# A cross-attention block on one core: the empty TensorE instructions taken out of a software-pipelined step, and its rows put in another order

## The chip, the cores and the metric

The kernel runs on one core of a Trainium2 chip. That core has five engines that run on their own and meet through semaphores: TensorE (PE, whose weight loads the profile lists apart as PEld), VectorE (DVE), ScalarE (ACT), GpSimd (POOL), and SyncE (SP), which here only issues DMAs. The metric is the device time of one launch in microseconds (us). The time before the change is the median of three runs.

## The reference

128 sequences of 128 tokens, 256 features, all in float32. The queries come from `x`, keys and values from `ctx_1024`; 16 heads of 16 features; the mask lets a token see only earlier ones, and the first token's attention is set to zero. Then an output projection, a residual and a layer norm, a ReLU network with 1024 hidden features, a residual and a second layer norm.

```python
q = (query @ Wq + bq);  k = (key @ Wk + bk);  v = (values @ Wv + bv)      # 16 heads of 16
scores = einsum('bhqd,bhkd->bhqk', q, k) / sqrt(16)
scores = where(j < i, scores, -1e30);  attn = softmax(scores);  attn[:, :, 0, :] = 0
ctx = einsum('bhqk,bhkd->bhqd', attn, v)
x = layer_norm(query + ctx @ Wo + bo, ln1_g, ln1_b)
out = layer_norm(x + relu(x @ W1 + b1) @ W2 + b2, ln2_g, ln2_b)
```

## The kernel before

**Pairs and steps.** The work is cut into 64 pairs of sequences. A step handles one pair's attention scores and, beside them, later parts of earlier pairs: step `p` computes the scores and the softmax of pair `p`, the queries and keys of pair `p+1`, the values of `p`, the weighted sum and the output projection of `p-2`, the first hidden layer of `p-3` or `p-4`, the second of `p-4` or `p-5`, and the second layer norm of `p-6`. Pairs 0 to 6 are handled by functions written out one by one (`third` to `sixth`), pair 63 by `last_step` and what follows it. Pairs 7 to 62 run through `step(p)`, 56 times; the loop goes on for two more rounds in which only late rows are left.

**Order.** The engines' order is manual: each engine executes its instructions in the order in which the program states them. In `step` that order is the string `ORDER`. Each word is a key of `OPS`; `-1` or `-2` behind a word means that the row is run for the pair of one or two steps earlier. So `ORDER` fixes the order on all engines at once, and what an engine does is the sub-list of its own keys. Semaphores are set by the framework, from what reads and writes what.

**The keys that matter here.**

- `weigh` (PE, lines 574 and 584): the probabilities times the values, 96 small matmul records, into PSUM bank 7. `context` (DVE, lines 600 and 605): three instructions that take bank 7, multiply by the inverse sums and write `cxT`.
- `scores` (PE, line 428): 64 records into all eight banks, in eight groups. Strips 2 and 3 of the array go first into banks 4 and 5, strips 0 and 1 into banks 0 and 1, and so on; the last two groups are those of strips 0 and 1 into banks 6 and 7.
- `maskB2`, `maskB3`, `maskA` (DVE, lines 452 and 444): bank 4, bank 5, banks 6 and 7. `add0` to `add3`, `max0` to `max3` (DVE, lines 1873 and 1879): mask and row maximum in banks 0 to 3. `eh0` to `eh7` and `el0` to `el7` (ACT, line 920): the exponentials of two heads each with their sums. `recip`, `turni` (DVE, lines 499 and 504): the inverse sums and their transposition; `turn0` to `turn2` (DVE, line 521): transposition of the probabilities; `turnx` (line 1935): of the normed rows. `br0` to `br3` (SP, line 540): sixteen DMAs that bring what was transposed from `turned` to `brought`, across partitions.
- Products by seven multiplications in place of eight (Strassen-Winograd), each of which has rows on PE and a chain of evacuations behind it. `v1` to `v4`, `o1` to `o4`, `q1` to `q4`, `k1` to `k4` (values in bank 4, output projection in bank 5, queries in bank 7, keys in bank 3): the row with 1 has three products, with 2 two, with 3 and 4 one. `h1` to `h7` (first hidden layer, banks 0, 1 and 2) and `w1` to `w7` (second layer, bank 6): one product of four matmuls each. A float32 matmul of 128x128x128 is two records, so a row `h` or `w` has eight records and a step has 168 such records beside `weigh` and `scores`.
- The evacuations add into, or copy out of, the same banks: `ok ok2 oa ob or` and `wk wk2 wa wb wr` (DVE, line 1327), `ka kb kr` (DVE, lines 1256, 1259, 1262), `qa qb qr` (DVE), `va vb vf vr` (DVE), `hk hk2 hk5` (ACT, lines 1402 to 1408), `hb ha hf` (DVE, lines 1414, 1411, 1417), `re0` (DVE, line 1431) and `re1` to `re3` (ACT, line 1433, ReLU out of banks 0 and 1), `ro0` to `ro3` (ACT, line 1421), `ks` and `ks2` (ACT line 1267 and POOL line 1272: keys spread over two halves, after `kr`). The sums that Strassen needs are built on POOL: `hs`, `xs`, `oc`, `cc`, `xc`.
- In the loop a product that adds onto an earlier one in the same bank stands behind the evacuation that reads the earlier one: `h4` behind `ha`, `h7` behind `hk2`, `k3` behind `kk2`.

**Empty instructions.** Behind each row of products, `step` puts some empty TensorE instructions (line 240, `nc.tensor.nop`): the dictionary `EMPTY` gives 4 or 5 for an `h` or `w` row and 2 or 3 for the others, 104 in a step. `LEAD` could put some ahead of a step and is empty.

Of the kernel before, what the change touches and what calls it, by code (L numbers as in the profile page):

```python
# [19 lines left out]
def tile_cross_attention_block(  # L20
# [83 lines left out]
    def weight(w, name):  # L104
        n = w.shape[0] // P
        t = const.tile([P, n, w.shape[1]], F32, tag=name, name=name)
        nc.sync.dma_start(t, w.rearrange("(k p) n -> p k n", p=P))
        return t
# [18 lines left out]
    wk = weight(Wk, "wk")  # L127
# [28 lines left out]
    w1 = weight(W1, "w1")  # L156
# [3 lines left out]
    w2 = weight(W2, "w2")  # L160
# [77 lines left out]
    def empty(n):  # L238
        for _ in range(n):
            nc.tensor.nop(hint="pad", nofuse=True)  # L240
# [1819 lines left out]
    for n in range(3):  # L2060
        OPS[f"turn{n}"] = lambda p, n=n: turn(p, n < 2, n % 2)

    ORDER = """
        weigh re0-2 res1-2 turn2-1 re2-2 re3-2 re1-2 context norm2-1 scores hs2-1 turni-1 vs-1
        maskB3 br2 add0 oc0 o1 ro0-2 maskB2 oc2 maskA ro2-2 finish1-1 v1 ro3-2 max0 ro1-2 q1 ok
        vk0 eh1 oc1 lowmax w1-1 hs0-1 qk br3 w2-1 vk1 add1 eh0 xs2-1 max1 el6 v2 hs1-1 stats2
        w5-1 eh3 add3 oc3 h2-1 eh2 max3 br1 hs3-1 wk-1 vk2 el5 o2 tokc-1 v3 eh7 xc2-1 h1-1 ok2
        add2 xc3-1 eh6 max2 cc0 q2 res0 vf el4 o3 br0 va w3-1 ob hk-1 oa vb eh4 cc1 w6-1 hb-1
        xs0-1 el0 cc2 o4 k1 wk2-1 xs1-1 qk2 or tokx el7 finish2-1 load w7-1 stats1 eh5 q3 means
        v4 kk h6-1 qa xc0 wb-1 el1 cc3 qb k2 deviations vr el3 wa-1 h5-1 turn1 kk2 loadx hk2-1  # L2070
        w4-1 xs3-1 store-1 norm1 turn0 addbo k3 h7-1 hk5-1 ka kb el2 xc1 turnx q4 k4 h3-1 ha-1
        kr qr h4-1 ks recip ks2 hf-1 wr-1
    """.split()

    EMPTY = {'w1': 5, 'h1': 4, 'w2': 5, 'h2': 5, 'w3': 5, 'h3': 4, 'w4': 5, 'h4': 5, 'w5': 5, 'h5': 4, 'w6': 5, 'h6': 5, 'w7': 4, 'h7': 5, 'v1': 3, 'o1': 2, 'q1': 2, 'k1': 3, 'v2': 2, 'o2': 2, 'q2': 3, 'k2': 2, 'v3': 2, 'o3': 3, 'q3': 2, 'k3': 3, 'v4': 2, 'o4': 2, 'q4': 3, 'k4': 2}
    LEAD = {}

    def step(p):

        empty(LEAD.get(p, 0))  # L2080
        for key in ORDER:
            key, late = (key.split("-") + ["0"])[:2]
            q = p - int(late)
            if FIRST <= q < NP - 1:
                OPS[key](q)
                if key in EMPTY:
                    empty(EMPTY[key])

    FIRST = 7

# [50 lines left out]
    for p in range(FIRST, NP - 1 + late):  # L2141
        step(p)
# [4 lines left out]
    p = NP - 1  # L2147
# [124 lines left out]
    means = small.tile([P, 2, 2], F32, tag="mvl", name="mv_last", bufs=1)  # L2272
# [83 lines left out]
```

## Time and profile before

| what | us |
|---|---|
| median of three runs (1507.5 to 1510.52) | 1508.35 |
| the profiled execution, its own time | 1508.16 |
| its span, first to last instruction | 1506.2 |
| busy: PE 1478.2, PEld 1405.8, DVE 1418.2, ACT 1294.9, POOL 1317.1 | share of the span 98, 93, 94, 86, 87% |

The profile is one execution. A busy share is an average over stages; rows of the timeline give start and length of one instruction (or of several alike that follow each other, with their count), and in square brackets the idle time before it with what ended it. PE rows are matmul records whose ends are modelled, so the distance between starts says more than their lengths. DVE and ACT instructions overlap a little with the next on the same engine, so here too starts are compared. The chain of waits is followed back from the last instruction: at each step to what released it.

### The profile page before, as it was taken

The page shows a single profiled execution, that of the slowest core. Times are in us where ns is not written, and L with a number is a line of the kernel's source. Part 1 is how long each engine was busy: PE and PEld are TensorE (multiplying, and loading weights), DVE is VectorE, ACT ScalarE, POOL GpSimd, SP SyncE. Part 2 cuts the span into 40 slices and gives each one's busy share as a digit, 9 for nine tenths or more (in the row PEclk, how much of TensorE's full clock was granted, in tenths as well). Part 3 has the DMA queues.
Part 4 walks back from the last instruction along what each step waited for, and adds up shares of the span by engine and source line. Part 5 has one row for each costly group of instructions (what it writes and reads, how often), then busy time and mean ns, then how long its engine had stood idle before and what let it go on. Part 6 is the DMA issues. An engine that isn't in the chain of part 4 may idle for free.

```text
span 1506.2 us, 62177 instructions
## 1 busy us (share of the span) xinstructions
PE 1478.2 (98%) x20711; PEld 1405.8 (93%) x20711; DVE 1418.2 (94%) x3397; ACT 1294.9 (86%) x5445; POOL 1317.1 (87%) x1877
## 2 busy tenths in 40 slices
PE   9998899999999999999999999999999999999898
PEld 7887899999999999999999999999999999999888
DVE  7997899999999999999999999999999999999567
ACT  6568799999999999999999899999999999999553
POOL 6876798999999899899899899899899899899667
PEclk9999799999999999999999999999999999999999
DMA  9366666766666666676665676676676676665251
GB/s 199 86 125 136 141 147 135 150 136 137 147 152 137 144 139 139 142 153 141 139 145 132 142 159 133 141 148 133 139 161 139 134 149 137 137 153 121 52 133 50
DMA packets 351320, 205.66 MB, mean 137 GB/s; under 512 B 277808, under 2 KB 319024, under 8 KB 351024
## 3 DMA queue, kind: packets, MB, share of 16 engines
q1 hardware_dynamic: 348736, 199.58, 61.7%
q8 instruction: 188, 3.08, 1.0%
q10 hardware_dynamic: 2288, 2.11, 0.6%
q14 instruction: 108, 0.88, 0.2%
HBM read 55.06 MB, written 18.09 MB: 49 GB/s over the span
## 4 chain that ended last, share of the span: by engine, by line
PE 32%; DVE 29%; SPq 16%; POOL 7%; ACT 7%; DMA 5%; issue 4%; DVEq 0%; POOLq 0%; ACTq 0%
PE banks L1175 19%; SPq L540 15%; DVE turned L521 9%; PE banks L1392 5%; ACT hT L1433 4%; PE banks L428 4%; DMA brought<-turned 3%; DVE hT L1411 2%; POOL kT L1272 2%; POOL hS L1868 2%; DVE t L1327 2%; DVE hT L1431 2%; DVE bsa L1900 1%; DVE kr L1259 1%; DVE xT L277 1%
## 5 line engine op out<-in xcount | busy, mean ns | idle before, releaser
L920 ACT ACTIVATE sm<-banks,nmx 128x128 f32<-128x128 f32 x944 | 352.4, 418 | 7.5 <-DVE nmx L903 7.5
L920 ACT ACTIVATE sm<-sm,nmx 128x64 f32<-128x64 f32 x944 | 344.8, 416 | 0.0
L920 ACT ACTIVATION_READ_ACCUMULATOR sm<-sm,nmx 128x1 f32 x944 | 251.8, 267 | 0.0
L920 ACT ACTIVATION_READ_ACCUMULATOR sm<-banks,nmx 128x1 f32 x944 | 242.4, 257 | 0.0
L521 DVE STREAM_TRANSPOSE turned<-sm 128x1024 f32<-128x1024 f32 x186 | 222.5, 1222 | 6.0 <-DMA brought<-turned 4.2
L1175 PE MATMUL banks<-wt,hS 128*128 128x128 f32 x1344 | 178.5, 276 | 0.4 <-DVE t L1327 0.4
L1392 PE MATMUL banks<-xS,w1t 128*128 128x128 f32 x1344 | 177.3, 275 | 0.0
L1868 POOL TENSOR_TENSOR hS<-hT 128x512 f32<-128x512 f32 x112 | 142.9, 1276 | 30.5 <-ACT hT L1433 29.6
L1175 PEld LDWEIGHTS banks<-wt,hS 128*128 128x128 f32 x1344 | 164.4, 193 | 0.6 <-DVE t L1327 0.6
L1392 PEld LDWEIGHTS banks<-xS,w1t 128*128 128x128 f32 x1344 | 163.5, 192 | 0.0
L1879 DVE TENSOR_REDUCE nmx<-banks 128x4 f32<-128x512 f32 x224 | 153.8, 687 | 5.7
L428 PE MATMUL banks<-kT,qT 32*64 32x256 f32 (+1 forms) x3840 | 123.7, 335 | 6.2 <-DVE t L1446 0.8
L428 PEld LDWEIGHTS banks<-kT,qT 32*64 32x64 f32 x3840 | 90.0, 132 | 31.2 <-ACT hT L1433 17.2
L1392 PE MATMUL banks<-brought,w 128*128 128x128 f32 x896 | 118.3, 275 | 0.0
L1175 PE MATMUL banks<-w,hT 128*128 128x128 f32 x896 | 110.8, 276 | 3.4 <-ACT hT L1421 2.0
L1433 ACT ACTIVATE hT<-banks,b1e_c 128x256 f32<-128x256 f32 x168 | 67.4, 472 | 50.9 <-DVE hT L1431 50.9
L1175 PEld LDWEIGHTS banks<-w,hT 128*128 128x128 f32 x896 | 105.4, 193 | 4.2 <-ACT hT L1421 2.4
L1392 PEld LDWEIGHTS banks<-brought,w 128*128 128x128 f32 x896 | 109.2, 192 | 0.0
L1272 POOL TENSOR_TENSOR kT<-kr,half 128x512 f32<-128x512 f32 x56 | 58.2, 1040 | 52.6 <-DVE kr L1262 52.6
L1421 ACT ACTIVATE hT<-hT,b1e_c 128x256 f32<-128x256 f32 x224 | 95.6, 497 | 0.7
L1873 DVE TENSOR_TENSOR banks<-banks,neg 128x256 f32<-128x256 f32 x224 | 94.0, 420 | 0.2
L691 ACT ACTIVATE x<-t,nb,sd 128x256 f32<-128x256 f32 x126 | 69.0, 596 | 23.7 <-POOL nb L1919 12.0
(330 smaller groups left out, 4947.4 us busy)
## 6 DMA issues: line engine op xcount, KB each, us to landing
brought<-turned SPq DMA_DIRECT2D x936, 128.0 KB, 2.4
out_dram<-t SPq DMA_DIRECT2D x63, 256.0 KB, 4.8
xb<-in_x_dram SPq DMA_DIRECT2D x124, 128.0 KB, 3.7
cb<-in_ctx_dram SPq DMA_DIRECT2D x124, 128.0 KB, 3.7
x<-in_x_dram SPq DMA_DIRECT2D x31, 512.0 KB, 5.7
brought<-turned SPq DMA_DIRECT2D x40, 96.0 KB, 2.2
w<-in_L_xattn_W_dram SPq DMA_DIRECT2D x2, 1024.0 KB, 8.3
brought<-turned ACTq DMA_DIRECT2D x8, 128.0 KB, 5.0
```

Of the source, the lines that this page charges most:

```text
L428: nc.tensor.matmul(st["sps", hi][r][s * HP : (s + 1) * HP, m * 2 * n : (m + 1) * 2 * n].rearrange("p (e j) -> p e j", e=2), st["qT"][strip ...
L521: nc.vector.transpose(turned[:, :, at : at + 256].rearrange("p j (n a) -> p n j a", a=32), states[p]["sm", hi].rearrange("p h j -> p (h j) ...
L540: queue.dma_start(brought_all[32 * j : 32 * j + 32, i, at], turned_all[32 * i : 32 * i + 32, j * ROW + at.start : j * ROW + at.stop],)
L920: nc.scalar.activation(sm[:, h, :], src, AF.Exp, bias=nmx[:, h : h + 1], scale=1.0, **({"accum_out": st["su"][:, at : at + 1]} if summed e ...
L1175: nc.tensor.matmul(out, left(k) if self.depth > 1 else left, right(k) if self.depth > 1 else right, start=(n == 1 and k == 0), stop=(k == ...
L1272: nc.gpsimd.tensor_tensor(self.kT[:, :, 1, :], self.k, half[:, 1:2, None].to_broadcast([P, KC, TP]), ALU.mult)
L1392: nc.tensor.matmul(ps[:, i * P : (i + 1) * P].rearrange("p (n a) -> p n a", a=32), left(i), right, start=(n in (1, 2, 5) and i == 0), stop ...
L1421: nc.scalar.activation(self.hT[:, f, at], self.hT[:, f, at] if src is None else src, AF.Relu, bias=b1e_c[:, f : f + 1], scale=1.0,)
L1433: nc.scalar.activation(out, src, AF.Relu, bias=bias, scale=1.0)
L1868: nc.gpsimd.tensor_tensor(c[:, n], left, right, how)
L1873: nc.vector.tensor_tensor(ps[:, :, HP:], ps[:, :, HP:], neg[:, 1, None, :].to_broadcast([P, 4, HP]), ALU.add)
L1879: nc.vector.tensor_reduce(states[p]["nmx", 1][:, 4 * b : 4 * b + 4], banks[:, b].rearrange("p (n j) -> p n j", j=P), AX.X, ALU.max, negate ...
```

## The change

The dictionaries `EMPTY` and `LEAD` and the calls of `empty` in `step` go: 104 TensorE instructions in each of 56 steps. `ORDER` is replaced by another order of the same keys. The lag of some keys changes, so that the same work stands on the other side of a step's border: `re0`, `re1`, `res1`, `turn2`, `turni` and `norm2` move from the start of a step to the end of the one before; `hf`, `wr`, `ks`, `ks2` and `xc1` move from the end of a step to the start of the next; `load` and `res0` come a step later than before, `xc2` a little earlier. On PE `v1` now comes ahead of `o1`, and the last rows are `h7 q4 v4 k3 h4 k4 h3` (before: `k3 h7 q4 k4 h3 h4`). On DVE the end of a step is `ha kb ka turnx qr re0 vr kr turn1`, and the next begins with `hf wr context maskB2 add0 maskB3 maskA` (before: it ended with `ka kb turnx ha kr qr recip hf wr` and the next began with `re0 turn2 context turni maskB3 add0 maskB2 maskA`).

```diff
-        weigh re0-2 res1-2 turn2-1 re2-2 re3-2 re1-2 context norm2-1 scores hs2-1 turni-1 vs-1
-        maskB3 br2 add0 oc0 o1 ro0-2 maskB2 oc2 maskA ro2-2 finish1-1 v1 ro3-2 max0 ro1-2 q1 ok
-        vk0 eh1 oc1 lowmax w1-1 hs0-1 qk br3 w2-1 vk1 add1 eh0 xs2-1 max1 el6 v2 hs1-1 stats2
-        w5-1 eh3 add3 oc3 h2-1 eh2 max3 br1 hs3-1 wk-1 vk2 el5 o2 tokc-1 v3 eh7 xc2-1 h1-1 ok2
-        add2 xc3-1 eh6 max2 cc0 q2 res0 vf el4 o3 br0 va w3-1 ob hk-1 oa vb eh4 cc1 w6-1 hb-1
-        xs0-1 el0 cc2 o4 k1 wk2-1 xs1-1 qk2 or tokx el7 finish2-1 load w7-1 stats1 eh5 q3 means
-        v4 kk h6-1 qa xc0 wb-1 el1 cc3 qb k2 deviations vr el3 wa-1 h5-1 turn1 kk2 loadx hk2-1
-        w4-1 xs3-1 store-1 norm1 turn0 addbo k3 h7-1 hk5-1 ka kb el2 xc1 turnx q4 k4 h3-1 ha-1
-        kr qr h4-1 ks recip ks2 hf-1 wr-1
+        weigh ks-1 ks2-1 re3-2 hf-2 re2-2 vs-1 wr-2 context scores hs2-1 ro0-2 br3 maskB2 ro2-2
+        add0 oc0 ro1-2 maskB3 v1 xc1-1 ro3-2 maskA o1 max0 hs0-1 vk1 q1 lowmax eh0 br2 w1-1 oc2
+        eh1 xs0-1 add1 tokc-1 w2-1 oc1 vk0 qk xc3-1 max1 el4 xs1-1 w5-1 add2 oc3 eh2 add3 hs1-1
+        h2-1 max2 br0 eh3 max3 v2 el6 res0-1 ok h1-1 wk-1 eh7 tokx o2 hs3-1 vk2 eh4 q2 br1 ok2
+        v3 stats2 hk-1 w6-1 finish1-1 eh5 hb-1 o3 qk2 vb w3-1 el2 vf addbo ob oa eh6 q3 o4 wk2-1
+        h6-1 va el0 qa cc0 or stats1 cc1 el7 loadx w7-1 cc3 qb load-1 el5 means xs2-1 k1 wa-1
+        el1 deviations wb-1 h5-1 turn0 el3 w4-1 kk cc2 recip hk2-1 turn2 xc2 k2 xc0 hk5-1 h7-1
+        finish2-1 kk2 turni norm1 q4 v4 ha-1 xs3-1 k3 store-1 norm2 res1-1 kb h4-1 ka turnx k4
+        qr h3-1 re0-1 vr kr re1-1 turn1
...
-    EMPTY = {'w1': 5, 'h1': 4, 'w2': 5, 'h2': 5, 'w3': 5, 'h3': 4, 'w4': 5, 'h4': 5, 'w5': 5, 'h5': 4, 'w6': 5, 'h6': 5, 'w7': 4, 'h7': 5, 'v1': 3, 'o1': 2, 'q1': 2, 'k1': 3, 'v2': 2, 'o2': 2, 'q2': 3, 'k2': 2, 'v3': 2, 'o3': 3, 'q3': 2, 'k3': 3, 'v4': 2, 'o4': 2, 'q4': 3, 'k4': 2}
-    LEAD = {}
-
     def step(p):
 
-        empty(LEAD.get(p, 0))
         for key in ORDER:
             key, late = (key.split("-") + ["0"])[:2]
             q = p - int(late)
             if FIRST <= q < NP - 1:
                 OPS[key](q)
-                if key in EMPTY:
-                    empty(EMPTY[key])
```

## The prediction

> **What bounds the kernel now.** I first read the busy shares, then the chain of waits, then one step of the timeline, engine by engine.
>
> ```profile
> PE 1478.2 (98%) x20711; PEld 1405.8 (93%) x20711; DVE 1418.2 (94%) x3397; ACT 1294.9 (86%) x5445; POOL 1317.1 (87%) x1877
> ```
>
> Two engines are nearly full, so the shares alone don't say which one sets the time. The chain does:
>
> ```profile
> 722.65 2.28 DVE turned L521 x2
> 731.48 5.35 PE banks L1175 x46
> 739.28 2.47 PE banks L1175 x22
> 745.13 2.28 DVE turned L521 x2
> ```
>
> It changes between PE and DVE in each step, and a step takes 745.13 - 722.65 = 22.48 us. So neither engine's sum sets the step, but a loop through both. The step's PE rows show where it closes.
>
> ```profile
> 705.41 0.43 PE L574 MATMUL banks<-brought,vd 128*32 128x64 f32 x16
> ...
> 706.89 2.11 PE L428 MATMUL banks<-kT,qT 32*64 32x128 f32 x64
> 708.94 0.71 PE L1175 MATMUL banks<-wo,cxT 128*128 128x128 f32 x4
> 709.49 0.39 PE L1175 MATMUL banks<-wot,oc 128*128 128x128 f32 x2
> ...
> 717.31 1.06 PE L1175 MATMUL banks<-w,hS 128*128 128x128 f32 x8
> 718.20 1.06 PE L1175 MATMUL banks<-wt,hS 128*128 128x128 f32 x8
> ```
>
> ```profile
> 707.40 1.35 PEld L428 LDWEIGHTS banks<-kT,qT 32*64 32x64 f32 x56 [0.31 <-ACT hT L1433]
> 708.94 0.52 PEld L1175 LDWEIGHTS banks<-wo,cxT 128*128 128x128 f32 x4 [0.19 <-DVE sm L452]
> ```
>
> From 709.49 to `w6` at 718.20 lie 78 records in 8.71 us, 0.1117 us each, without a gap; the first four of `o1` take 0.55, 0.10 more than that. PE loses time in `scores` alone: 0.31 us until `re1` has left banks 0 and 1, and 0.19 until `maskB3` has left bank 5, which is where DVE holds it.
>
> ```profile
> 708.50 0.38 DVE L452 TENSOR_TENSOR sm<-banks,neg 128x256 f32<-128x256 f32 x1
> ...
> 719.29 0.29 DVE L1327 TENSOR_TENSOR t<-banks,x1b 128x128 f32<-128x128 f32 x1
> ...
> 722.17 0.28 DVE L1311 COPY vz<-banks 128x128 f32<-128x128 f32 x1
> 722.37 0.28 DVE L1327 TENSOR_TENSOR t<-banks,t 128x128 f32<-128x128 f32 x1
> 722.57 2.36 DVE L521 STREAM_TRANSPOSE turned<-sm 128x1024 f32<-128x1024 f32 x2
> 724.88 0.29 DVE L1256 TENSOR_TENSOR kr<-banks,kr 128x128 f32<-128x128 f32 x1
> 725.08 0.41 DVE L1259 TENSOR_TENSOR kr<-banks,kr 128x256 f32<-128x256 f32 x1
> 725.41 0.70 DVE L1935 STREAM_TRANSPOSE turned<-x 128x512 f32<-128x512 f32 x1
> 726.04 0.65 DVE L1411 TENSOR_TENSOR hT<-banks,hT 128x512 f32<-128x512 f32 x1
> 726.61 0.33 DVE L1262 TENSOR_SCALAR kr<-banks,bk_c 128x128 f32<-128x128 f32 x1
> 726.87 0.34 DVE L1226 TENSOR_SCALAR qT<-banks,bqs_c 128x128 f32<-128x128 f32 x1
> 727.12 0.34 DVE L499 RECIPROCAL rs<-su 128x32 f32<-128x32 f32 x1
> 727.38 0.63 DVE L1417 TENSOR_TENSOR hT<-banks,hT 128x512 f32<-128x512 f32 x1
> 727.93 0.28 DVE L1327 TENSOR_TENSOR t<-banks,x1b 128x128 f32<-128x128 f32 x1
> 728.12 0.47 DVE L1431 TENSOR_SCALAR hT<-banks,b1e_c 128x256 f32<-128x256 f32 x1
> 728.51 1.23 DVE L521 STREAM_TRANSPOSE turned<-sm 128x1024 f32<-128x1024 f32 x1
> 729.67 0.38 DVE L600 TENSOR_TENSOR cxT<-banks,brought 128x256 f32<-128x256 f32 x1
> 729.98 0.47 DVE L605 TENSOR_TENSOR cxT<-banks,brought 128x124 f32<-128x124 f32 x2
> ```
>
> `w6` ends at 718.20 + 0.89 = 719.09 and `wk2` starts 0.20 later. From there DVE runs without a break, through all the rows shown, up to `maskB3` of the next step; it ends 22.48 after 708.50 + 0.38 = 708.88, and `o1` starts 0.06 after it. That is the loop of today: `o1` to `w6` on PE, `wk2` to `maskB3` on DVE. The same rows give the measures for the new order: 0.20 us from the end of a product to the DVE instruction that waits for it, 0.06 back, and DVE's distances from start to start.
>
> **The change part by part.**
>
> **The 104 empty instructions.** I put them at nothing.
>
> ```profile
> L240 PEldq NOP  x6292: 13/13/13, 1.1 to 1491.8; - x197
> ```
>
> Five stand behind `w3`, yet `w6` starts 0.89 after it, eight records' time, as between any two rows. The sequencer takes them while the array works off what is queued; that queue is their cover. Without it 104 of 13 ns would be worth 1.35 us a step, 72 us in all; that is the bound on one side. I see nothing by which taking them out costs time.
>
> **Work that moves but isn't on the loop.** No instruction of another engine is added or removed, so every engine's sum stays. The sixteen DMAs of `br` now start behind `context` and not behind `turni`:
>
> ```profile
> SPq L540 <- DVE turned L504: 397.0, 55, 9.6
> ```
>
> SP sat 397.0/55 = 7.2 us a step waiting for it, so its queue has room for `loadx`, `load` and `store`, which follow; what they bring is wanted a step later. The old `add`-`max` pairs, each of which waits for itself on DVE, are pulled apart; DVE gains there, but in the middle of the step, where in the new order it waits for products anyway. I put both at nothing; what ACT and POOL do in between I take as covered by their 14 and 13% of idle time.
>
> **What waits for what.**
>
> ```profile
> 727.04 0.72 ACT L1267 ACTIVATE kT<-kr,half 128x512 f32<-128x512 f32 x1 [0.64 <-DVE kr L1262]
> 728.63 1.20 ACT L1433 ACTIVATE hT<-banks,b1e_c 128x256 f32<-128x256 f32 x3 [0.87 <-DVE hT L1431]
> ```
>
> `re2` (the first of the three on ACT) waits for `re0` on DVE, though both only read, and other columns: what touches the same bank on another engine waits, in the program's order. And `ks` starts 727.04 - 726.61 = 0.43 after `kr`.
>
> **The new loop.** In the new order `v1` is the first product behind `scores`; from it to `h7` PE has 144 records. Behind `h7` comes `ha`, and behind `ha`, in order on DVE, all that ends in `context`. The last two groups of `scores` overwrite bank 7, where `context` reads, so they wait for it, and `v1` stands behind them on PE, with everything else that PE has. The terms:
>
> 1. `v1` to the end of `h7`: 144 x 0.1117 + 0.10 = 16.18.
> 2. To the start of `ha`: 0.20.
> 3. DVE from `ha` to `context`: `ha` 0.57, `kb` 0.33, `ka` 0.20, `turnx` 0.63, `qr` 0.25, `re0` 0.39, `vr` 0.20, `kr` 0.26, `turn1` 2.31/2 = 1.16, `hf` 0.55, `wr` 0.19: together 4.73.
> 4. `kb` reads bank 3, where `k3` stands ahead of it in the program, in other columns: as with `re2`, it waits. `k3` ends `q4 v4 k3`, six records or 0.67, behind `h7`, and 0.20 later `kb` may start, 0.87 behind `h7`; `ha` lets it start at 0.20 + 0.57 = 0.77. So 0.10 more.
> 5. `context`: 729.67 to 729.98 + 0.47 = 730.45, so 0.78; release 0.06.
> 6. The last two groups of `scores`:
>
> ```profile
> L428 PE MATMUL banks<-kT,qT x3840: 267/374/684, 81.5 to 1425.7; 32*64 32x128 f32 x97, 32*64 32x256 f32 x95
> ```
>
> 128 columns more take 374 - 267 = 107 ns. Two groups are four records of 128 columns one behind the other: 3 x 0.107 + 0.267 = 0.59. A third of an unhindered `scores` (below) would be 0.53; with a first-row cost like that of `o1` it is 0.69. I take 0.59.
>
> Sum: 16.18 + 0.20 + 4.73 + 0.10 + 0.78 + 0.06 + 0.59 = 22.64 us, 0.16 more than 22.48.
>
> Is PE early enough to feel that wait?
>
> ```profile
> 144.46 1.67 PE L428 MATMUL banks<-kT,qT 32*64 32x128 f32 x64
> 146.06 0.71 PE L1175 MATMUL banks<-wo,cxT 128*128 128x128 f32 x4
> ```
>
> Here, in the first step of the loop, `scores` waits for nothing and takes 1.60. Counted from the start of `ha`: `h4` may start at 0.65 + 0.06 = 0.71; `h4 k4 h3` are 18 records or 2.01; `weigh` starts 0.09 behind a row like these and takes 1.48 (705.41 to 706.89); and 1.60 - 0.59 = 1.01 of `scores` later PE stands before bank 7, at 0.71 + 2.01 + 0.09 + 1.48 + 1.01 = 5.30. DVE releases it at 4.83 + 0.78 + 0.06 = 5.67, so PE has to wait. ACT is no earlier than DVE: `kr` starts at 2.67, `ks` at 3.10, `re3` and `re2` follow it (0.72, a third of 1.20 and 0.47) and end by 4.66, and from there strips 0 and 1 need what they need today, 708.94 - 707.40 = 1.54, less the last 0.59: 5.67 with the release, or some 0.1 less, since ACT's instructions overlap. So two paths of about one length hold `v1`.
>
> The step repeats in full 53 times (56, less the first two, while late rows are missing, and the last): 53 x 0.16 = 8.5 us. Against the profiled execution's own 1508.16 that is 1516.7; the median of the runs is 0.2 higher, which I leave out.
>
> A rule of the Trainium skill bears on term 4. PSUM — Partial Sum Buffer, section "PSUM bank collisions raise a hardware error", says that no two engines may be in the same bank and quadrant at once, reads included, and that one guards by bank and not by address; the row of `re2` agrees. By it the step is 22.64. Guarded by address, `kb`, whose columns `k2` has finished, would not wait for `k3`: 22.54, and 1508.16 + 53 x 0.06 = 1511.3.
>
> **The rivals.**
>
> *`context` comes in time and the step gets shorter.* If DVE and ACT have bank 7 and banks 0 and 1 free when PE gets there, `v1` waits only for `maskB2`, one instruction behind `context`: that is 0.31 + 0.47 - 0.08 (the overlap seen between rows) = 0.70, its own 0.38 and 0.06. Terms 5 and 6 then become 1.14 in place of 1.43: 22.35, and 1508.16 - 53 x 0.13 = 1501.3. It decides as soon as the eleven rows of term 3, and `kr` with `ks` among them, take about 0.4 less than I sum (5.67 against 5.30). For it: `re0` and `turn2` no longer stand between `wr` and `context`, and `re1` is taken before the step's border. Against it: `turn1`, with 1.16 the longest row, stands there in their place. Were PE to meet no wait at all, its step would be 22.48 - (2.05 - 1.60) = 22.03 (2.05 is 706.89 to 708.94), and the time 1484.3.
>
> *It makes no difference.* The loop comes out within 0.06 of 22.48, for instance with no wait at `kb` and 0.53 for the groups (22.48): 1505 to 1511.
>
> *A wait between `hf` and `re2`.* Both write `hT`; the new order is `re3 hf re2`. If one waits for the other, `re2` starts behind `hf`, at 0.57 + 0.10 + 0.33 + 0.20 + 0.63 + 0.25 + 0.39 + 0.20 + 0.26 + 1.16 + 0.63 = 4.72 after `ha`, takes 0.47, and `scores` goes on from there to `v1` as after the 0.31 of today, in 708.94 - 707.40 = 1.54: 6.73 for terms 3 to 6 in place of 6.26, so 23.11, and 1541.6. Against it: they write other columns.
>
> *The empty instructions did hold something*: up to 72 us faster, by the bound above. Nothing in the rows speaks for it.
>
> **How the numbers follow.** The loop of 22.64: 0.62. No difference: 0.15. The shorter step: 0.16, and 0.02 for the empty instructions. `re2` behind `hf`: 0.05. The likeliest one's own range is 22.54 to 22.74 a step, 1511 to 1522. The range for 8 in 10 takes in no difference and part of the shorter step: 1503 to 1523. 0.2% or 3 us is about what a measurement of this kernel can tell from no change; all of the loop's range lies above 1511.2, so slower has 0.67, the same 0.15, faster 0.18.
>
> **What would show it.** In the changed profile: the step in the chain at 22.6; no row in which PE waits 0.31 for line 1433, and in its place weight loads of line 428 that wait for DVE `cxT`, 0.1 to 0.4 each; `ha` (line 1411) waiting for PE line 1392 in nearly every step, and DVE's busy time spread over a longer span; records still 0.112 apart. It is wrong if `ha` starts long after `h7`, if `v1` starts right behind `maskB2`, or if PE stands still elsewhere, ahead of `k2` or `h7` for ACT above all.

## The result and the profile after

The changed kernel takes 1528.55 us (median of 4 runs, 1528.02 to 1529.03) against 1508.82 in the runs of the kernel before beside it: 1.0130 times as long, 95% interval 1.0112 to 1.0148. The forecast was slower, 1516.7, with a range up to 1523. The direction came, but the loss is 19.7 us where 8.4 were forecast. The profiled execution has a span of 1526.0.

The busy shares tell as little as before:

```profile
PE 1488.0 (98%) x20711; PEld 1415.2 (93%) x20711; DVE 1410.1 (92%) x3397; ACT 1299.1 (85%) x5445; POOL 1320.8 (87%) x1877
```

The chain of waits (start, duration, what) has a repeating piece of TensorE, the 42 records from `v1` on. Its starts give the step:

```profile
651.31 4.88 PE banks L1175 x42
674.95 4.88 PE banks L1175 x42
697.65 4.88 PE banks L1175 x42
...
743.23 4.89 PE banks L1175 x42
765.93 4.88 PE banks L1175 x42
```

Two things stand in these rows. The common step is 765.93 - 743.23 = 22.70 us, where 22.64 was forecast and 22.48 was the step of before. And the steps are no longer alike: from 651.31 to 674.95 it is 23.64. Before, 49 of 53 took 22.48 or 22.49.

One common step, first on TensorE and then on DVE, answers to the rows of the prediction's new loop (start, duration, engine and line):

```profile
720.44 0.71 PE L1175 MATMUL banks<-wv,cT 128*128 128x128 f32 x4
...
735.73 1.08 PE L1392 MATMUL banks<-xS,w1t 128*128 128x128 f32 x8
...
737.66 1.16 PE L1392 MATMUL banks<-brought,w1t 128*128 128x128 f32 x8 [0.18 <-DVE hT L1411]
...
741.34 1.89 PE L428 MATMUL banks<-kT,qT 32*64 32x128 f32 x64
743.15 0.71 PE L1175 MATMUL banks<-wv,cT 128*128 128x128 f32 x4
```

```profile
736.91 0.69 DVE L1411 TENSOR_TENSOR hT<-banks,hT 128x512 f32<-128x512 f32 x1
...
741.71 0.41 DVE L600 TENSOR_TENSOR cxT<-banks,brought 128x256 f32<-128x256 f32 x1
742.04 0.47 DVE L605 TENSOR_TENSOR cxT<-banks,brought 128x124 f32<-128x124 f32 x2
```

`v1` starts at 720.44, `ha` 16.47 later, `context` 4.80 after `ha`; `context` ends 0.80 after its start, and the next `v1` comes 0.64 behind that. `h7` is the row at 735.73, `h4` the one at 737.66. From the start of `scores` to `v1` it is 1.81, not the 1.60 of a step without a wait. That is the loop as forecast, and each term can be set beside its row (further down).

A long step looks like this in TensorE's weight loads (in brackets the idle time before a row, and what ended it):

```profile
672.12 1.43 PEld L428 LDWEIGHTS banks<-kT,qT 32*64 32x64 f32 x58
674.50 0.20 PEld L428 LDWEIGHTS banks<-kT,qT 32*64 32x64 f32 x6 [0.95 <-issue]
```

In the middle of `scores` TensorE stands still for 0.95 us, six loads before the end, and the releaser is "issue": the engine waited for nothing that the profile shows, no semaphore and no other engine. The list of waits (total, times, longest) puts all of these together:

```profile
PEld banks L1392 <- DVE hT L1411: 23.1, 56, 1.3
...
PEld banks L428 <- issue: 5.2, 11, 0.9
```

In the kernel before, that second row is 0.5 us in all. One thing that would not show as a releaser is an instruction that has not come yet. The page counts the transfers on the instruction queues (packets, MB, share); here is one of these queues, of before and of after:

```profile
q8 instruction: 188, 3.08, 1.0%
```

```profile
q8 instruction: 166, 2.72, 0.8%
```

Both are 16.4 KB a packet (3.08 MB / 188). TensorE has two instructions for each of its 20,711 records, a weight load and a product. With the 6292 empty instructions that line 240 had before, that is 47,714 / 188 = 254 a packet; with the 468 that it still has in after, outside `step`, 41,890 / 166 = 252. With the waits of its sequencer (560 and 782, other empty instructions included) it comes to 257 both times; at 256 an instruction is 16,384 / 256 = 64 bytes. So this queue is TensorE's program, in blocks of 256 instructions.

Now count a step. `weigh` has 96 records, `scores` 64, the seven products of `v`, `o`, `q` and `k` together 56, `w` and `h` 56 each: 328, so 656 instructions. With the 104 empty ones and 8 waits of the sequencer, a step of before has 768, which is three blocks exactly; each step of before began at the same place of a block. The new step has 656 and 12 waits, 668, and this place moves by 156 in each step. That gave theory A: **the empty instructions held the code blocks in step with the loop**, and the long steps are those in which a block ends at a bad place. Theory B was the prediction's: they cost nothing and hold nothing.

Counted along the trace of after, with the place of `weigh`'s first instruction in its block of 256 (from the first instruction in the trace, so that the true start of a block may lie elsewhere), the 53 regular steps sort themselves:

```
place of weigh    steps   mean step   shortest   longest   (us)
  0 to 127          26      22.77       22.70     23.08
128 to 159           7      23.24       22.70     23.63
160 to 191           6      22.99       22.75     23.66
192 to 223           8      22.82       22.70     23.05
224 to 255           6      22.74       22.70     22.82
```

The 18 steps with a place of 122 to 210 are together 5.3 us longer than the others would be.

### The profile page after: what moved, and what is told of

It is laid out like the page before. It is cut to its first block, busy times and chain, and to the rows that moved or that the text cites. A ratio compares the mean times of both kernels' runs of the same rounds, so it can differ in the third digit from the quotient of the medians.

```text
span 1526.0 us, 56681 instructions
## 1 busy us (share of the span) xinstructions
PE 1488.0 (98%) x20711; PEld 1415.2 (93%) x20711; DVE 1410.1 (92%) x3397; ACT 1299.1 (85%) x5445; POOL 1320.8 (87%) x1877
## 4 chain that ended last, share of the span: by engine, by line
PE 79%; DVE 8%; POOL 4%; ACT 3%; SPq 2%; issue 2%; DMA 2%; DVEq 0%; POOLq 0%; ACTq 0%
PE banks L1175 40%; PE banks L1392 22%; PE banks L428 7%; PE banks L584 3%; DVE hT L1411 3%; PE banks L574 2%; SPq L540 2%; DVE turned L521 2%; ACT sm L920 1%; PE banks L858 1%; PE banks L960 1%; DMA brought<-turned 1%; PE banks L1072 1%; PE banks L288 1%; POOL sm L464 1%
## 5 line engine op out<-in xcount | busy, mean ns | idle before, releaser
L920 ACT ACTIVATE sm<-sm,nmx 128x64 f32<-128x64 f32 x944 | 330.6, 425 | 0.0
L920 ACT ACTIVATION_READ_ACCUMULATOR sm<-sm,nmx 128x1 f32 x944 | 261.3, 277 | 0.0
L521 DVE STREAM_TRANSPOSE turned<-sm 128x1024 f32<-128x1024 f32 x186 | 226.1, 1219 | 7.8 <-DMA brought<-turned 5.7
L1879 DVE TENSOR_REDUCE nmx<-banks 128x4 f32<-128x512 f32 x224 | 146.1, 672 | 0.0
L1433 ACT ACTIVATE hT<-banks,b1e_c 128x256 f32<-128x256 f32 x168 | 72.4, 465 | 75.3 <-DVE hT L1431 54.5
L428 PE MATMUL banks<-kT,qT 32*64 32x128 f32 (+1 forms) x3840 | 118.8, 336 | 4.8 <-issue 2.3
L428 PEld LDWEIGHTS banks<-kT,qT 32*64 32x64 f32 x3840 | 93.8, 132 | 20.7 <-issue 5.2
L1873 DVE TENSOR_TENSOR banks<-banks,neg 128x256 f32<-128x256 f32 x224 | 89.9, 425 | 0.7 <-PE banks L428 0.4
L1900 DVE BATCH_NORM_STATS2 bsa<-t 128x6 f32<-128x256 f32 x224 | 83.2, 414 | 0.0
```

What stands on the lines that cost most here:

```text
L428: nc.tensor.matmul(st["sps", hi][r][s * HP : (s + 1) * HP, m * 2 * n : (m + 1) * 2 * n].rearrange("p (e j) -> p e j", e=2), st["qT"][strip ...
L521: nc.vector.transpose(turned[:, :, at : at + 256].rearrange("p j (n a) -> p n j a", a=32), states[p]["sm", hi].rearrange("p h j -> p (h j) ...
L920: nc.scalar.activation(sm[:, h, :], src, AF.Exp, bias=nmx[:, h : h + 1], scale=1.0, **({"accum_out": st["su"][:, at : at + 1]} if summed e ...
L1433: nc.scalar.activation(out, src, AF.Relu, bias=bias, scale=1.0)
L1873: nc.vector.tensor_tensor(ps[:, :, HP:], ps[:, :, HP:], neg[:, 1, None, :].to_broadcast([P, 4, HP]), ALU.add)
L1879: nc.vector.tensor_reduce(states[p]["nmx", 1][:, 4 * b : 4 * b + 4], banks[:, b].rearrange("p (n j) -> p n j", j=P), AX.X, ALU.max, negate ...
```

## The experiments

**Only the empty instructions out, the old order kept.**

```
-    EMPTY = {'w1': 5, 'h1': 4, 'w2': 5, ...
+    EMPTY = {}
```

> The order of before, with nothing but the 104 empty instructions of a step taken out. Theory A (code fetch): TensorE's program comes in blocks of 256 instructions of 16 KB, and a step of before is 768 instructions, three blocks, so a block begins at the same place of every step; without the empty instructions a step has 664, the place drifts, and in the steps in which a block ends inside weigh or scores TensorE waits for code. In the trace of after these stalls sum to about 7.4 us; the order of before has a wait of 0.31 us inside scores that can hide some of each, so 3 to 7 us more: 1511 to 1516. Theory B (the empty instructions cost and hold nothing, as predicted): 1508.4, within 1 us, and a step that repeats at 22.48 us.

Measured: 1518.51 against 1508.28, ratio 1.0069 (1.0054 to 1.0084). Taking out work that costs nothing makes the kernel 10.2 us slower. The loss is more than theory A's sum; theory B is out.

```profile
PEld banks L428 <- ACT hT L1433: 17.8, 55, 0.6
PEld banks L428 <- issue: 8.3, 19, 1.0
```

The wait for `re1`, which I had thought would hide part of the stalls, is there in full (17.8 us, 17.2 before), and the stalls come on top. In this trace 25 steps with a place under 122 take 22.51 in the mean, nearly the old 22.48; the 28 with a place of 122 to 250 are together 10.8 us longer.

**The new order with three whole blocks a step, in a good and in a bad place.** Both kernels have the order of after and 100 empty instructions in a step, so 768 again. They differ in one thing: the first two steps of the loop, in which the second kernel has 122 empty instructions more.

```
+    EMPTY = {...}              # before's, with w2, w5, h2 and h7 one less
+    MORE = {7: -2}             # the bad place: {8: 3}
...
+                if key in EMPTY:
+                    empty(EMPTY[key] + MORE.get(p, 0))
```

> The new order with 100 empty instructions in a step, so that a step is 768 instructions again, and placed so that weigh begins 42 instructions behind the start of a block. Theory A: no step stalls for code; steps of 22.70 us, every fourth 22.81, and 1528.6 - 7.4 = 1521 (1519 to 1523). Theory B: as the new order without them, 1528.5, with the irregular steps of 23.0 to 23.7 still there.

> The same kernel with 122 empty instructions moved elsewhere in the second step of the loop, by which weigh begins 164 instructions behind the start of a block in every step, where the trace of after shows its longest stalls. Theory A: nearly every step stalls, 0.2 to 0.9 us each, 0.5 in the mean over 53 steps: 1521 + 27 = 1548 (1532 to 1568), with a gap among the rows of scores for which the trace names no releaser. Theory B: the same time as the other placement, to 0.1%.

Measured: 1523.31 in the good place (ratio 1.0101, 1.0086 to 1.0116) and 1542.59 in the bad one (1.0228, 1.0212 to 1.0243). Two kernels whose loops are the same, instruction by instruction, from the third step on are 19.3 us apart. In the good place TensorE waits 0.5 us in all for "issue" ahead of rows of `scores`; in the bad one

```profile
PEld banks L1392 <- DVE hT L1411: 35.6, 56, 1.7
PEld banks L428 <- issue: 15.2, 45, 0.8
```

45 times TensorE stalls there. The first row shows a second loss, 35.6 in place of 22.0 us in the good place: `ha` itself comes late. The list of DVE's waits shows what holds DVE ahead of it:

```profile
DVE turned L521 <- DMA brought<-turned: 18.2, 23, 3.3
```

`turn0` waits 23 times for the last of the `br` transfers to land (2 times and 3.5 us in the good place). Worked out over 40 steps of each trace, the last `br` transfer of a step lands 2.40 us behind its issue in the good place and 3.55 in the bad one. In the bad place a code packet starts 12.6 to 15.3 us behind `weigh`, 14.4 in the middle, which is when that transfer is under way. Transfer by transfer the two go together. In the good place 152 of the `br` transfers had a code packet start within 1.6 us after their issue; 150 of these took over 3 us to land, 3.67 in the middle, and of the other 664 only 24 did, with 2.38 in the middle. In the bad place it was 199 of 200 against 36 of 616. The slow transfers are there in both kernels, but in the bad place the last one, on which `turn0` waits, is among them. How the packet holds them up is not shown.

The bad place shows what a stall is, in one step's weight loads:

```profile
676.00 0.27 PEld L574 LDWEIGHTS banks<-brought,vd 128*32 128x32 f32 x16
...
677.48 1.10 PEld L428 LDWEIGHTS banks<-kT,qT 32*64 32x64 f32 x46
679.11 0.44 PEld L428 LDWEIGHTS banks<-kT,qT 32*64 32x64 f32 x18 [0.53 <-issue]
```

`weigh` starts at 676.00, and a code packet starts at 676.31 by the records of that queue. TensorE goes on at 679.11, 2.80 behind the packet's start. In the trace of after, the seven gaps of over 0.3 us in `scores` end 2.2 to 2.75 us behind a packet's start, 2.49 in the middle. `weigh` and `scores` together are 320 instructions in 1.48 + 1.60 = 3.08 us, so a block that falls into them is used up in about 2.46, before the next is there; and in these seven the packet starts only 0.04 to 1.24 us behind the first instruction of the block, 0.61 in the middle. Elsewhere 256 instructions are 128 records of 0.1117, 14.3 us. In the good place one packet starts 2.0 to 3.8 us ahead of `weigh` and the next 1.7 to 2.5 behind its start: the block that ends in `weigh` began in slow code.

The count itself shows that it is the end of a block. Of the waits for "issue" inside `scores` in the regular steps, all 7 of after and all 40 of the bad place end at place 193 of the count by 256, and all 19 of the old order without empty instructions at 194, wherever `weigh` began. From `weigh`'s first instruction, place 193 is 151 instructions away in the good place and then 407, when `scores` is over.

**The old order in the bad place.**

```
-    LEAD = {}
+    MORE = {7: 2, 8: 2}
...
-                    empty(EMPTY[key])
+                    empty(EMPTY[key] + MORE.get(p, 0))
```

> The order of before with all its empty instructions and 92 more in two steps alone, so that weigh begins 164 instructions behind the start of a block and not 72. Theory A: each step loses some of the 0.5 us of the new order, less what its own wait of 0.31 in scores hides: 0.1 to 0.6 a step, 1514 to 1540. Theory B: 1508.4 and at most 1 us more.

Measured: 1547.30, ratio 1.0256 (1.0239 to 1.0273): 39 us for 92 empty instructions more, out of 6292, and beyond my estimate. 52 times TensorE stalls in `scores`, in the regular steps always at place 194:

```profile
PEld banks L428 <- issue: 25.1, 52, 0.8
PEld banks L428 <- ACT hT L1433: 19.7, 55, 0.6
```

**As many empty instructions as before, in the new order.** It has `EMPTY` as in before, 104, and `MORE = {7: -2, 8: 2}`, so 772 instructions in a step.

> The new order with all 104 empty instructions that before has, four more a step than makes three blocks. Theory A (code fetch): the place of weigh in its block moves by four in a step, from 106 behind the start of a block up to 322, that is 66 of the next, and crosses the bad places, 122 to 210, in some 22 of the steps and in one stretch: steps of 22.7 at first, then 22 of them 0.4 longer, then 22.7 again, together 1523.3 + 9 = 1532 (1527 to 1538). If it is the number of empty instructions that helps and not their making three whole blocks: 1523.

Measured: 1538.09, ratio 1.0201 (1.0180 to 1.0222): 14.8 us more than with 100, and slower than with none. The steps came in a stretch, as theory A has it. The first four and the last thirteen are 22.7 to 22.9 long; of those between, the 33 over places 122 to 250 take 23.20 in the mean, and three more, up to place 6 of the next block, 23.06 to 23.69. That stretch is longer than the one up to 210 that I had read from after, and the 23 steps within that one are 0.5 longer and not 0.4; so the 6 us by which I was low. It is not the number of empty instructions that helps; whole blocks do, where they end in a good place.

**Does the loop go through `context`?** `tokc`, 0.61 us on DVE, is moved into the tail behind `kr`, in the kernel with the good place.

```
-        eh1 xs0-1 add1 tokc-1 w2-1 oc1 ...
+        eh1 xs0-1 add1 w2-1 oc1 ...
...
-        qr h3-1 re0-1 vr kr re1-1 turn1
+        qr h3-1 re0-1 vr kr re1-1 turn1 tokc
```

> The new order with 100 empty instructions in its good placement (1523.3), with tokc (0.61 us on DVE) taken from the middle of the step, where DVE waits for products soon after, to the tail, between turn1 and hf. kr, and with it the way by ks and re2 to scores, stays as early as it is; only context, maskB2 and what follows get later. Theory A (the loop goes from ha to context and on to v1): 0.61 more in each step, 23.3, and 1523.3 + 54 x 0.61 = 1556 (1550 to 1560), and the wait inside scores grows by as much. Theory C (the loop goes by ks and re2, or by ACT's exponentials, and context has room): less than 0.3 a step, under 1540.

Measured: 1553.99, ratio 1.0306 (1.0289 to 1.0323), 30.7 more than without the move. In the chain of waits, two steps of `scores`:

```profile
682.71 2.41 PE banks L428 x54
...
706.03 2.41 PE banks L428 x56
```

The step is 23.32, 0.61 more than 22.71. DVE's sum in a step is the same; only the place of `tokc` changed, and all of it came through: from the start of `scores` to `v1` it is 2.41 in place of 1.82. TensorE's wait for `context` now stands in the list, where the good place has none:

```profile
PEld banks L428 <- DVE cxT L605: 15.3, 54, 0.3
```

The loop by `ha`, `context` and `v1` is shown.

**`wr` behind `maskB2`**, to make that tail shorter.

```
-        weigh ks-1 ks2-1 re3-2 hf-2 re2-2 vs-1 wr-2 context scores hs2-1 ro0-2 br3 maskB2 ro2-2
+        weigh ks-1 ks2-1 re3-2 hf-2 re2-2 vs-1 context scores hs2-1 ro0-2 br3 maskB2 wr-2 ro2-2
```

> The new order with 100 empty instructions in its good placement (1523.3), and wr (0.20 us on DVE) taken from ahead of context to behind maskB2. Theory A (the loop of the prediction: v1 to h7 on TensorE, ha to context on DVE, the last groups of scores): context can start at 4.63 behind ha in place of 4.80, limited by weigh, which ends 4.43 behind ha; a step is 22.54 in place of 22.71, and 1523.3 - 53 x 0.17 = 1514.3 (1512 to 1517). Theory C (what holds the step is the wait that the list shows as the longest, TensorE for ha ahead of h4, 0.4 us a step, or the chain of exponentials on ACT): nothing is gained, 1522 to 1524.

Measured: 1551.25, ratio 1.0293 (1.0277 to 1.0310). The edit was a bad one: `wr` reads bank 6, and `scores` writes it. So `wr` adds scores in place of its product (that part of the result is changed), and on DVE it has to wait for `scores`:

```profile
DVE t L1327 <- PE banks L428: 22.4, 54, 0.4
```

It says nothing for or against the loop; the run above took its place.

**What held before?** `qa` ahead of `wk2`, in the old order, to fill DVE's idle time of 0.14 there (it starts 0.20 behind the end of `w6`).

```
-        ... cc2 o4 k1 wk2-1 xs1-1 ...
+        ... cc2 o4 k1 qa wk2-1 xs1-1 ...
```

> The kernel before with one DVE instruction moved: qa (0.18 us, its product ended 2 us earlier) ahead of wk2, so that DVE does something useful in the 0.20 us in which it waits for w6. If the loop of before is the one that the prediction named (o1 to w6 on TensorE, wk2 to maskB3 on DVE), it is opened at this place: 0.15 to 0.20 less a step, 56 steps, 1498 to 1500. If that loop was misread: 1508, within 0.1%.

Measured: 1506.91 against 1507.68, ratio 0.9994 (0.9985 to 1.0003): no difference. (`qa` stands ahead of `q3` here, so it adds an unfinished sum; the queries are changed.) DVE's wait went, and a new one came, 50 times:

```profile
DVE kr L1256 <- PE banks L1175: 8.1, 50, 0.4
```

`ka` now waits 0.16 for `k3`: TensorE is not earlier. A move that keeps the result, `tokx` ahead of `hb`, and one that opens TensorE's side, `h4` ahead of `h3` with `re0` and `wr` ahead of `turn2` and `hf`, were tried apart and together:

```
-        ... oa vb eh4 cc1 w6-1 hb-1 xs0-1 el0 cc2 o4 k1 wk2-1 xs1-1 qk2 or tokx el7 ...
+        ... oa vb tokx eh4 cc1 w6-1 hb-1 xs0-1 el0 cc2 o4 k1 wk2-1 xs1-1 qk2 or el7 ...
```

```
-        weigh re0-2 res1-2 turn2-1 re2-2 re3-2 re1-2 context ...
+        weigh res1-2 turn2-1 re2-2 re3-2 re1-2 hf-2 context ...
...
-        ... q4 k4 h3-1 ha-1 kr qr h4-1 ks recip ks2 hf-1 wr-1
+        ... q4 k4 ha-1 h4-1 kr qr h3-1 ks recip ks2 re0-1 wr-1
```

> The kernel before with tokx (0.62 us on DVE, it needs no product) moved ahead of hb, so that both 0.13 us waits there (hb on hk, wk2 on w6) are filled. If the loop that the prediction named for before were the only one, a step would lose up to 0.33: 1490 to 1495. If TensorE's own row, from scores without a gap to k3 and from there by ka, ha, re0 and re1 back to scores, is a second loop of the same length (as the run with qa moved showed, where ka began to wait 0.16 for k3): no change, 1506 to 1509.

> The kernel before with h4 ahead of h3 on TensorE, and re0 and wr ahead of turn2 and hf on DVE, so that re0 to re3 end before scores wants banks 0 and 1: the 0.31 us wait of scores goes. If two loops of one length hold before, this opens only TensorE's, and maskB3 on DVE, which is as late as it was, takes the wait over (0.19 becomes about 0.5): 1506 to 1509.

> Both edits together. With both loops open a step is held by DVE's sum or by TensorE's, 22.15 to 22.25 in place of 22.48: 1508 - 56 x 0.28 = 1492 (1489 to 1498). If something else of the same length holds the step (ACT, POOL or the br transfers): 1504 to 1509.

Measured: `tokx` alone 1508.20, ratio 1.0003 (0.9993 to 1.0013); `h4` alone 1551.80, 1.0295 (1.0277 to 1.0313); both 1552.22, 1.0299 (1.0276 to 1.0323). The first was as expected by the second branch; the other two were misses. With `tokx` moved, DVE has no wait at `hb` and `wk2` any more, and stands 0.38 a step for `q3` instead:

```profile
DVE qT L1216 <- PE banks L1175: 21.5, 56, 0.5
```

With `h4` ahead of `h3`, in the run of both, TensorE stands 42.9 us in all before `h4`, waiting for `ha`, and DVE stands behind it:

```profile
DVE hT L1431 <- PE banks L1392: 31.1, 55, 1.3
```

`re0` waits 0.55 a step for `h4`, in DVE's fullest stretch. So I found no version faster than the kernel before.

**The loads ahead of the last four `br` transfers**, in the new order with the good place.

```
-        h2-1 max2 br0 ... vk2 eh4 q2 br1 ok2
+        h2-1 max2 br0 ... vk2 eh4 q2 loadx load-1 br1 ok2
```

> The new order with 100 empty instructions in its good placement (1523.3), and the loads of two later pairs put ahead of the last four of the sixteen br transfers on SP's queue, which they follow otherwise; they hold that queue for 3.3 to 4.4 us in a step. The prediction put the place of br at nothing because SP's queue has room: 1523. Theory D (the transfers are a path of their own: context, sixteen issues of 0.65 us, a landing of 2.4, turn0, ha): the trace shows turn0 starting 0.8 us in the mean behind the last landing, so 2.5 to 3.6 us more in each step and 1523 + 53 x 3 = 1682 (1650 to 1715).

Measured: 1923.79, ratio 1.2756 (1.2732 to 1.2781), 400 us more, beyond both expectations. The place on SP's queue matters, as theory D has it, but the size is no measure of the path. The load of `x` waits for `stats` on DVE, and now the transfers wait behind it:

```profile
SPq L99 <- DVE bsa L1900: 106.7, 27, 5.0
```

(37.9 us in 27 times in the good place without the move.) How much room the transfers have in the new order was not settled by this run.

## Why the prediction was right or wrong

**The 104 empty instructions: wrong, and this is the step that failed.** "I see nothing by which taking them out costs time" put them at nothing, with a bound on the side of a gain alone. The runs show a loss: 10.2 us in the old order, and 1528.55 - 1523.31 = 5.2 in the new. I had asked what their 13 ns cost, and found the cover, which was right: the common step is 22.71 with 100 of them in the good place and 22.70 without. I had not asked what they did to the instructions around them, which is to hold the ends of the code blocks at one place of the step. The row of 188 packets of 16.4 KB stood in the profile of before, and 768 could be counted. The rival "the empty instructions did hold something" had the wrong sign, since it took them for a brake. Of the 11.8 us by which the forecast was too low, these are 5.2; the other 6.6 lie in the sizes of the new loop. With the good place alone the time, 1523.3, would still have stood at the upper end of the range.

A rule of the Trainium skill bears on this, in Runtime: NRT & Kernel Launch, section "Instruction fetch mechanics". It says that an engine's code comes in blocks of 16 KiB, 256 instructions, the next while the current one runs, and that crossing a boundary is "mostly hidden". The block agrees with 3.08 MB in 188 packets; "mostly hidden" does not hold where 320 instructions take 3.08 us, and cost up to 39 us here.

**The new loop: right in its path, a little small in its size.** Its terms, forecast and measured (all in us):

```
v1 to the start of ha         16.18 + 0.20 = 16.38      16.47
ha to the start of context     4.73 + 0.10 =  4.83       4.80
context                                       0.78       0.80
its release, two groups        0.06 + 0.59 =  0.65       0.64
step                                         22.64      22.71
```

The term that was too small is the second: `h7` ends 735.73 + 0.89 = 736.62, and `ha` starts 0.29 later, not the 0.20 read at `w6` and `wk2`. From `v1` to `h7` it is 15.29, as 136 records and the 0.10 make it.

Without the stalls, that is with the good place, the new order takes 1523.3: 15.0 more than before, where 8.4 were forecast for it. Of the 6.6 between, 53 x 0.07 = 3.7 lie in the step; every fourth step is 0.11 longer again, 22.81 (13 x 0.11 = 1.4). It follows a step in which `ks` started 0.19 later, and loses the time between `v1` and `ha`, ahead of `o4`, `k2` and `h7`; why is not shown. The rest is in a few single steps, two of them of 23.06.

**`kb`'s wait for `k3`**: it starts 0.61 behind `ha` where DVE alone would allow 0.57, and its place fits the end of `k3` and 0.20. The wait is there but is 0.04, not 0.10, since `ha` came a little later behind `h7`.

**Two paths of about one length: not quite.** `re2` ends 4.50 behind `ha` in place of 4.66, so that way would let `v1` start at 6.1; `context` does at 6.24. (The forecast's own terms, 3.10 + 0.72 + 0.40 + 0.47, add up to 4.69 and not 4.66.) The run with `tokc` moved lengthened the one and not the other, and the step followed it in full.

**The work that moves, put at nothing**: mostly right where the code blocks end well. The room of the `br` transfers is small, but in after DVE waits 5.7 us in 4 times for them (4.2 in 2 times before). In the bad place it is 18.2.

**The loop of before: half read.** The fills at `wk2` let DVE come earlier and won nothing: it then waited for TensorE, 0.16 at `ka` for `k3` or 0.38 at `qa` for `q3`. So TensorE's own row, from `scores` to `k3`, is as long to within some hundredths. That it closes back to `scores` by `re0` is my reading, and no run shows it. This didn't enter the sum, which was made against the measured step.

**The rivals.** `context` did not come in time, so no step was 22.35. `re2` did not wait for `hf`: it ends at 4.50, ahead of `hf`'s end. Of the signs, the 22.6 in the chain and the 0.111 between records came, and the wait of 0.31 for line 1433 went (0.2 us in one time). The waits of 0.1 to 0.4 on `context` did not show as rows of their own before `tokc` was moved: they lie inside `scores`, from whose start to `v1` it is 1.81 and not 1.60. `ha` does wait for `h7` in nearly every step, though the list seems to deny it:

```profile
DVE hT L1411 <- ACT x L691: 6.4, 37, 0.2
DVE hT L1411 <- PE banks L1392: 4.6, 11, 2.2
```

A wait for several semaphores stands in the list under the one that came last there, and rows of up to 0.15 us are left out. In 46 of the 53 regular steps DVE stands 0.16 to 0.54 us idle ahead of `ha`, and in 49 of them `ha` starts 0.38 behind the start of `h7`'s last record, to within 0.003. From the end of line 691 the distance is not fixed: 0.07 to 0.14 in the common steps of the good place. In the step shown above DVE came later than in most and stood only 0.03.

## What to carry to other kernels

Before an instruction that does nothing is taken out or put in, count the engine's instructions in a step of the loop and divide by the block in which its code comes, here 256. A step that is a whole number of blocks keeps each block's end at one place, and then the place decides: in the new order 768 instructions a step took 1523.3 or 1542.6 us, and 668 took 1528.6 between them. Any other number moves the place from step to step, by 156 or by 4 here, and so through the bad ones too. The worst place is where instructions are shortest: code that uses up a block in less time than a block takes to come, here about 2.5 us. A wait for "issue" in the middle of such a row, next to the count of code packets, is how the profile shows it.

And where several loops of a tuned kernel are equally long, the wait with the most microseconds in a list need not be the one that holds it. Lengthening a path by a known amount, as with `tokc`, tells more than filling a wait.

## What of the hardware was not expected

TensorE can run out of code in the middle of a straight row: gaps of 0.2 to 1.0 us, all at one place of the block, which ended 2.2 to 2.75 us behind the start of a code packet in after. Ninety-two empty instructions in two steps of 56 made the old order 39 us slower, and 122 in two steps the new one 19 us, by the place of the blocks alone. A transfer of the good place with a code packet starting within 1.6 us after its issue took 3.67 us to land, in the middle, where the others took 2.38; in the bad place it hit the last of the sixteen, on which DVE waits, in most steps.
